# A gated attention block on one core: when reads of DRAM scratch are emitted, and large transfers cut in four

## The chip, the core and the metric

The kernel runs on one core of a Trainium2 chip. The metric is the device time of one execution in microseconds (us). TensorE (PE) multiplies matrices, VectorE (DVE) and ScalarE (ACT) work on tiles, GpSimd (POOL) masks, and SyncE (SP) does nothing but issue transfers (DMAs). Each engine takes its instructions in the order of the program. An instruction whose inputs aren't there holds everything behind it on its engine; for SP that means every later transfer.

## The reference, cut to what matters

`x` has 2 batches of 1024 tokens with 512 features. All arithmetic is float32.

```python
xn = layernorm(x)
q, k, v = xn @ Wq.T + bq, xn @ Wk.T + bk, xn @ Wv.T + bv      # 32 heads of 16
s = causal_softmax(q @ k.T / 4) @ v @ Wo.T + bo
f = xn @ W_base.T + b_base + 2-of-8 routed low-rank part (A, B, W_gate)
out = x + s * silu(f)
```

## The kernel before

**Tiling.** A chunk is 512 tokens, so there are 2 x 2 chunks (b, c). Four groups of eight heads (oc = 0 to 3) per chunk give 16 units (b, oc, c). A unit's attention is cut into steps; the list `plan` holds 144 of them. The loop at the end of `direct` records for each step n the scores (`s<-qT,kT`, line 1542), the product of the exponentials with the values for step n-1 (`av<-pt,v`, line 1594), the mask, and then calls `fill(n)`.

**Order.** Nothing is scheduled at run time. `fill(n)` records as many other matmuls (line 228) as the step's share allows, taken from a list of tasks with due steps; then it runs through `later`, a list of (step, function) pairs, and runs those whose step has come; then it steps the tasks that cost TensorE nothing (loads, sums of weights, layernorm); last, `issue_parts` records loads of weight blocks. So the recorded step of a DMA sets only its place on SP's queue. When it really starts depends on everything in front of it there.

**Weights in seven products.** Value, gate and output projections and most query-key projections use a scheme of seven products in place of eight. It needs sums of blocks of the weights. `combine_task` (line 583) loads a whole 1 MB matrix (`load_whole`, line 140), makes the four block sums in place on DVE (`four_sums`), and stores the result to DRAM scratch as one 1 MB DMA, `kept<-w_gate` (line 597). Later `issue_parts` (line 617) loads blocks of 256 KB one at a time: `w<-in_wb_dram` straight from the weight, `wt<-kept` from the scratch. `qk_weights_task` (line 621) does the same for the query-key weights of one oc: two loads of 256 KB (`load_qk`, line 123), pairing on ACT, sums on DVE, one 1 MB store `kept<-wqk` (line 646); for batch 1 the tile is read back (line 626). The `wqk` tiles share two buffers, so a third tile (`wqk2`) can only be loaded when the last product that reads the tile in its buffer (`wqk1`, in step 17) is done.

**Other trips through DRAM scratch.** Turning the normalized tokens: `scr<-sq` (line 301) and four reads `xnT<-scr` (line 308). Turning the routed activations: `hscr<-hsq` and `hwT<-hscr` (lines 980, 987). The softmax denominators of a unit: `den<-oT`, `den<-avs` (line 1029), `dens<-den` (line 1034), a reciprocal on DVE, `back<-rc` (line 1037), `avs<-back` (line 1054), and then on DVE `rb<-avs` and a product with `oT`. Each read waits on SP for its write. The step in which a read is recorded is a fixed number of steps after the write's: one for `place` and `spread`, one or two for `collect` and `merge`.

**Around step 12 to 22**, where the gate projection of chunk (0, 0) begins, SP's recorded order is: step 12 `w_gate`, the two loads of `wqk2`, first gate block `w11`; step 13 `hwT` four times, `kept<-wqk0`, block `w21`; step 15 `back<-rc`; step 16 `avs<-back` twice, `kept<-w_gate`; step 17 `wt2<-kept`, `wt3<-kept`; step 19 the copies of kT; step 20 those of qT and `wt1`. The products of the gate stand in the steps 19 (`p1`), 20 (`p2`), 21 (`p6`, which reads `wt2`) and on.

Of the kernel before, what the change touches and what calls it, by code (L numbers as in the profile page):

```python
# [18 lines left out]
P = 128  # L19
# [40 lines left out]

@with_exitstack
def attn_gated_block(ctx: ExitStack, tc: tile.TileContext, *args):

    nc = tc.nc
    flag = ctx.enter_context(tc.tile_pool(name="flag", bufs=1))
    sound = flag.tile([1, 1], I32, name="sound")
    with ExitStack() as direct_ctx:
        direct(direct_ctx, tc, sound, *args)
    n = nc.values_load(sound[0:1, 0:1])
    with tc.If(n < P * NF, preferred_fallthrough_block=False):
        with ExitStack() as general_ctx:
            general(general_ctx, tc, *args)


def direct(ctx, tc, sound, x, wq, wk, wv, wo, wb, wa, wg, wB, bq, bk, bv, bo, bb, out):
# [11 lines left out]
    act = Metered(nc.scalar, 0.22, 1274)  # L94
    NB, L, _ = x.shape
# [19 lines left out]
    for t in range(TT):  # L115
        nc.sync.dma_start(out=first[t], in_=x[0, t * P : (t + 1) * P, :])

    def load_qk(oc):


        t = sb.tile([P, 4 * KC, P], F32, tag="wqk", bufs=2, name=f"wqk{oc}")
        for n, src in enumerate((wq, wk)):
            nc.sync.dma_start(
                out=t[:, (2 + n) * KC : (3 + n) * KC],
                in_=src.rearrange("(kc p) o -> p kc o", p=P)[:, :, oc * P : oc * P + P],
            )
        return t
# [12 lines left out]
    def load_whole(src, name):  # L140

        t = sb.tile([P, KC, D], F32, tag="xnT", bufs=3, name=name)
        nc.sync.dma_start(out=t, in_=src.rearrange("(kc p) o -> p kc o", p=P))
        return t

    def load_b(src, name):
        t = cst.tile([P, D], F32, name=name)
        nc.sync.dma_start(out=t, in_=src.partition_broadcast(P))
        return t
# [13 lines left out]
    def load_rest():  # L163


        def by_rows(w):
            return w.rearrange("(kc p) o -> p kc o", p=P)

        for dst, src in (
            (wag_sb[:, :, 0:ER], by_rows(wa)),  # L170
            (wag_sb[:, :, ER:], by_rows(wg)),
            (wB_sb, wB),
            (bb_sb, bb.partition_broadcast(P)),
            (bo_sb, bo.partition_broadcast(P)),
        ):
            nc.sync.dma_start(out=dst, in_=src)
# [87 lines left out]
    def layernorm_task(b, c):  # L264


        xt = chunk_tile(b, c)
        for i in range(NS):
            i0 = c * C + i * P
            nc.sync.dma_start(  # L270
                out=xt[i * SQ : (i + 1) * SQ],
                in_=x[b, i0 : i0 + P].rearrange("(t r) d -> r t d", r=SQ),
            )
        if b == 0:
            load_rest()
        tiles = [xt[:, t] for t in range(TT)]
        for _ in range(3 if b else 1):
            yield WAIT
        s = yield from statistics(tiles, True)
        if b:  # L280
            yield WAIT
        for t in range(0, TT, 2):
            normalize(tiles[t : t + 2], s[0][:, t : t + 2], s[1][:, t : t + 2])
            yield PAUSE
        if b:
            yield WAIT
        xnT = sb.tile([P, KC, C], F32, tag="xnT", bufs=3, name=f"xnT_{b}_{c}")
        for k0 in range(0, KC, 2):
            sq = sb.tile([P, 2, NS, TT, SQ], F32, tag="sq", bufs=1, name="sq")
            for t in range(TT):  # L290
                yield PAUSE
                ve.transpose(
                    out=sq[:, :, :, t],
                    in_=tiles[t][:, k0 * P : (k0 + 2) * P].rearrange(
                        "p (k q d) -> p k q d", k=2, q=NS
                    ),
                )
            scr = dram.tile([NS, SQ, 2, NS, TT * SQ], F32, tag="scr", name="scr")

            def store(sq=sq, scr=scr):  # L300
                nc.sync.dma_start(
                    out=scr.rearrange("i d k q m -> (i d) (k q m)"),
                    in_=sq.rearrange("p k q t r -> p (k q t r)"),
                )

            def place(k0=k0, scr=scr):
                for q in range(NS):
                    nc.sync.dma_start(
                        out=xnT[q * SQ : (q + 1) * SQ, k0 : k0 + 2].rearrange(
                            "d k (i m) -> d k i m", i=NS  # L310
                        ),
                        in_=scr[:, :, :, q].rearrange("i d k m -> d k i m"),
                    )

            if not b:
                store()
                place()
                yield WAIT
                continue
            later.append((now[0] + b, store))  # L320
            later.append((now[0] + b + 1, place))
            for _ in range(0 if k0 else 1 + b):
                yield WAIT
        xnTs[b, c] = xnT
        turned_at[b, c] = now[0] + b
# [137 lines left out]
    def place_keys(kT, low):  # L463
        for par in range(2):
            nc.sync.dma_start(out=kT[1 - par :: 2, par].bitcast(F32), in_=low[par::2])
# [15 lines left out]
    def place_queries(qT):  # L481
        for par in range(2):
            both = qT[:, 2 * par : 2 * par + 2].bitcast(F32)
            nc.sync.dma_start(out=both[1 - par :: 2], in_=both[par::2])
# [82 lines left out]
    combined, kept_at, sums, sums_at, issued_at, ended = {}, {}, {}, {}, {}, [0]  # L567
    made = [0] * len(stages)
    qk_kept, qk_ready, qk_done = {}, {}, {}
# [13 lines left out]
    def combine_task(name, given=None):  # L583

        src, bias = weights[name]
        w = given or load_whole(src, f"w_{name}")
        for _ in range(0 if given else 3):
            yield WAIT
        at = {
            (i, j): w[:, 2 * i : 2 * i + 2, BK * j : BK * j + BK]  # L590
            for i in range(2) for j in range(2)
        }
        yield from four_sums(at, {int(t[1]): at[p] for t, p in IN_PLACE.items()})
        kept = dram.tile([P, KC, D], F32, tag=f"kept_{name}", bufs=1, name="kept")
        ve.tensor_tensor(bias[:, BK:D], bias[:, BK:D], bias[:, 0:BK], ALU.subtract)
        yield WAIT
        nc.sync.dma_start(out=kept, in_=w)
        combined[name], kept_at[name] = kept, now[0]

        for _ in range(2):  # L600
            yield WAIT

    def issue_parts():
        while issued[0] < len(parts) and issued[0] - used[0] < NWP:
# [3 lines left out]
            if part[0] == "t" and now[0] < kept_at.get(name, now[0]) + 1:  # L608
                return
            w = sb.tile([P, 2, BK], F32, tag="wp", bufs=NWP, name=f"w{part}")  # L610
# [6 lines left out]
            nc.sync.dma_start(out=w, in_=src)  # L617
# [3 lines left out]
    def qk_weights_task(n):  # L621

        oc = n % KC
        if n >= KC:
            wqks.append(sb.tile([P, 4 * KC, P], F32, tag="wqk", bufs=2, name=f"wqk{oc}"))
            nc.sync.dma_start(out=wqks[n], in_=qk_kept[oc])
        else:
# [17 lines left out]
            yield WAIT  # L645
            nc.sync.dma_start(out=qk_kept[oc], in_=w)
            for _ in range(2):
                yield WAIT
        qk_ready.setdefault(n, now[0] + 2)
# [179 lines left out]
    def gate_task(k):  # L829
# [18 lines left out]
        def final(i, j):  # L848
# [20 lines left out]
            def store():  # L869
                nc.sync.dma_start(out=block_of(kept)(i, j), in_=g(i, j))  # L870
# [9 lines left out]
    def out_task(k):  # L880
# [10 lines left out]
        def load():  # L891
            i, j = order[len(xts)]
            xts[i, j] = sb.tile([P, 2, BK], F32, tag="xr", name=f"xr_{b}_{c}_{i}{j}")
            nc.sync.dma_start(out=xts[i, j], in_=block(x, i, j))
            gts[i, j] = sb.tile([P, 2, BK], F32, tag="gr", name=f"gr_{b}_{c}_{i}{j}")
            nc.sync.dma_start(out=gts[i, j], in_=g(i, j))

        def final(i, j):
# [7 lines left out]
            def store():  # L906
                nc.sync.dma_start(out=block(out, i, j), in_=y(i, j))
# [10 lines left out]
    def routed_task(b, c):  # L918
# [60 lines left out]
        def store():  # L979
            nc.sync.dma_start(  # L980
                out=scr.rearrange("i d q m -> (i d) (q m)"),
                in_=sq.rearrange("p q t r -> p (q t r)"),
            )

        def place():
            for q in range(NS):
                nc.sync.dma_start(
                    out=hwT[q * SQ : (q + 1) * SQ].rearrange("d i t r -> d i (t r)"),
                    in_=scr[:, :, q].rearrange("i d m -> d i m"),
                )  # L990

        later.append((now[0] + 1, store))
        later.append((now[0] + 2, place))
        hwTs[b, c] = hwT
        turned_at[b, c, "h"] = now[0] + 1
# [20 lines left out]
    def post(n, b, oc, c, avs):  # L1016
# [10 lines left out]
        def leave():  # L1027
            for par, t in enumerate((o, avs)):
                nc.sync.dma_start(
                    out=den[par].rearrange("s j w -> s (j w)"), in_=t[HD - par :: HP]  # L1030
                )

        def spread():
            nc.sync.dma_start(out=dens[:, u], in_=den.rearrange("a s j w -> (a s j) w"))

        def give_back(rc):
            nc.sync.dma_start(
                out=back.rearrange("a s (j w) -> (a s j) w", w=W), in_=rc
            )
            later.append((now[0] + 1, collect))  # L1040
# [11 lines left out]
        def collect():  # L1052
            for par in range(2):
                nc.sync.dma_start(out=avs[HD - par :: HP], in_=back[par])
            later.append((now[0] + 2, finish))
# [10 lines left out]
        later.append((n + 3, spread))  # L1066
        if wait:
            patient.extend((merge, finish))
        later.append((n + 4 + wait, merge))

    def post_tile(b, oc, c, t, avs):
# [17 lines left out]
        if posted.count(t) == 2:  # L1089
            turns.append((now[0] + 1, lambda: turn_last(b, c, t)))  # L1090

# [19 lines left out]
    def bases_task(b, c):  # L1111

        xt = sb.tile([P, TT, D], F32, tag="xnT", bufs=3, name="x_last")
        nc.sync.dma_start(
# [17 lines left out]
    def finish_tile(b, c, t, po):  # L1132
# [4 lines left out]
        nc.sync.dma_start(out=out[b, i * P : (i + 1) * P, :], in_=y)  # L1137
# [172 lines left out]
    for b in range(NB):  # L1310
        for c in range(NC):
# [10 lines left out]
            turned_ = lambda u=(b, c): now[0] > turned_at.get(u, now[0]) + (3 if u[0] else 2)  # L1322
# [13 lines left out]
            if not b and not c:  # L1336
# [14 lines left out]
                for n in range(2 * KC):  # L1351
# [4 lines left out]
                            and len(qk_ready) >= n  # L1356
                        ),
# [77 lines left out]
    def fill(n):  # L1435
# [3 lines left out]
        now[0], begun_at = n, spent  # L1439
        within = 0 <= n < len(plan)  # L1440
# [54 lines left out]
        for x in [x for x in later if x[0] <= n]:  # L1495
            if x not in later or x[0] == n and x[1] in patient and enough():
                continue
# [617 lines left out]
```

## Time and profile before

| what | value |
| --- | --- |
| runs | 558.41, 559.28, 560.47 us; median 559.28 us |
| profiled execution | 560.55 us, of which the span of the trace is 558.8 us |
| ACT busy | 351.2 us (63%) |
| DVE busy | 332.7 us (60%) |
| transfers | 79.16 MB, mean 142 GB/s |
| largest group | `pt<-s` on ACT, 288 instructions of 1024 ns |

The span is the time from the first to the last instruction in the trace. The profiled execution is one of its own: its time lies 1.27 us above the median, and 1.75 us of it lie outside the span. "Busy" is the sum of an engine's instructions; a wait is idle time of an engine with the instruction that ended it. In the trace's lines, DVE and ACT instructions have line 56, since a helper (`Metered`) records them; they are told apart by their tiles.

### The profile page before, as it was taken

The numbers are of one execution on the slowest core, as the hardware profiler recorded it, in microseconds if no ns is written. First come the engines' busy times: TensorE is split into PE (matmuls) and PEld (weight loads), VectorE is DVE, ScalarE is ACT, GpSimd is POOL, SyncE is SP. The second block draws the span as 40 slices with busy tenths as digits, with TensorE's granted clock in tenths as the row PEclk, the third lists the DMA queues.
The fourth block names the chain that finished last, engine by engine and source line by source line (L and its number), as shares of the span: only waits on it lengthen the run. The fifth ranks groups of instructions, "written<-read, shape, count | busy, mean of one in ns | idle before, by whom it ended". The sixth has DMA issues, their size and how long they took to land.

```text
span 558.8 us, 19435 instructions
## 1 busy us (share of the span) xinstructions
PE 540.5 (97%) x8411; PEld 280.2 (50%) x8411; DVE 332.7 (60%) x693; ACT 351.2 (63%) x389; POOL 115.9 (21%) x248
## 2 busy tenths in 40 slices
PE   8999999959999999999999999999999999999993
PEld 8435444524445554444645554454545554455651
DVE  4435587137567675566549765585267553648833
ACT  2537754645777676756657755756667777776640
POOL 2203401010213530130213430120113331020500
PEclk9999999979999999999999999999999999999998
DMA  8634370565564555741575544641124221652311
GB/s 266 170 112 174 120 228 3 184 235 192 153 157 143 222 174 167 209 144 60 167 198 177 171 156 134 225 142 41 60 78 137 79 83 46 230 168 81 97 40 46
DMA packets 65198, 79.16 MB, mean 142 GB/s; under 512 B 9560, under 2 KB 52576, under 8 KB 63696
## 3 DMA queue, kind: packets, MB, share of 16 engines
q1 hardware_dynamic: 65088, 77.83, 43.5%
q8 instruction: 68, 1.11, 0.8%
q14 instruction: 26, 0.21, 0.1%
q10 hardware_dynamic: 16, 0.00, 0.0%
HBM read 46.39 MB, written 19.37 MB: 118 GB/s over the span
## 4 chain that ended last, share of the span: by engine, by line
PE 92%; DMA 3%; DVE 2%; ACT 1%; issue 0%; SPq 0%; POOL 0%; ACTq 0%; POOLq 0%; DVEq 0%
PE av L1594 25%; PE p L228 23%; PE s L1542 18%; PE q L228 13%; PE pv L228 2%; PE po L228 2%; PE ph L228 2%; PE pq L228 1%; PE pk L228 1%; DMA back<-rc 1%; ACT pt L56 1%; DMA kept<-w_gate 1%; PE warm L183 1%; DMA wqk<-in_wk_dram 1%; PE pq_first L351 1%; PE h L228 1%
## 5 line engine op out<-in xcount | busy, mean ns | idle before, releaser
L56 ACT ACTIVATE pt<-s 128x1024 f32<-128x1024 f32 x288 | 290.2, 1024 | 158.7 <-PE s L1542 149.0
L1570 POOL TENSOR_SCALAR_AFFINE_SELECT pt<-pt 128x256 f32<-128x256 f32 (+1 forms) x224 | 108.0, 497 | 416.9 <-ACT pt L56 416.1
L1594 PE MATMUL av<-pt,v 128*32 128x512 f32 (+3 forms) x1680 | 157.2, 469 | 0.2 <-DVE v L56 0.2
L1542 PE MATMUL s<-qT,kT 32*128 32x512 f32 (+3 forms) x1616 | 108.7, 365 | 0.7 <-ACT pt L56 0.5
L1542 PEld LDWEIGHTS s<-qT,kT 32*128 32x128 f32 x1616 | 62.4, 184 | 59.8 <-issue 35.3
L1594 PEld LDWEIGHTS av<-pt,v 128*32 128x32 f32 x1680 | 41.6, 109 | 55.0 <-issue 39.1
L228 PE MATMUL p<-wt,asum 128*32 128x256 f32 x960 | 59.9, 386 | 6.2 <-DMA wt<-kept 6.2
L228 PE MATMUL q<-asum,wqk 128*32 128x256 f32 x832 | 51.3, 379 | 0.6 <-DVE qf L56 0.6
L228 PEld LDWEIGHTS p<-wt,asum 128*32 128x32 f32 x960 | 31.8, 112 | 36.0 <-issue 12.2
L228 PE MATMUL q<-xnT,wqk 128*32 128x256 f32 x624 | 39.5, 379 | 0.0
L228 PEld LDWEIGHTS q<-asum,wqk 128*32 128x32 f32 x832 | 26.7, 110 | 24.6 <-issue 6.9
L56 DVE TENSOR_TENSOR g<-p,g 128x512 f32<-128x512 f32 x20 | 13.8, 689 | 31.6 <-PE p L228 31.5
L228 PEld LDWEIGHTS q<-xnT,wqk 128*32 128x32 f32 x624 | 20.2, 110 | 18.4 <-issue 6.6
L56 DVE SCALAR_TENSOR_TENSOR kf<-q,kf 128x256 f32<-128x256 f32 x39 | 16.5, 424 | 21.2 <-PE q L228 20.5
L228 PE MATMUL p<-w,xnT 128*32 128x256 f32 x448 | 27.9, 379 | 0.0
L228 PEld LDWEIGHTS p<-w,xnT 128*32 128x32 f32 x448 | 15.7, 110 | 10.3 <-issue 3.3
L228 PE MATMUL p<-w,asum 128*32 128x256 f32 x320 | 20.7, 379 | 0.0
L228 PEld LDWEIGHTS ph<-wag_sb,xnT 128*32 128x32 f32 x512 | 15.2, 110 | 3.9 <-issue 3.3
L228 PE MATMUL po<-wo,oT 128*32 128x512 f32 x128 | 16.5, 593 | 0.4 <-ACT oT L56 0.4
L228 PE MATMUL ph<-wag_sb,xnT 128*32 128x136 f32 x512 | 16.6, 279 | 0.0
L56 DVE TENSOR_TENSOR x<-p,x 128x512 f32<-128x512 f32 x15 | 10.3, 687 | 10.3 <-PE p L228 10.2
L56 DVE TENSOR_TENSOR qT<-qf,qT 128x512 fp32r<-128x512 f32 x15 | 10.3, 684 | 9.8 <-ACT qT L56 9.8
(145 smaller groups left out, 555.7 us busy)
## 6 DMA issues: line engine op xcount, KB each, us to landing
wt<-kept SPq DMA_DIRECT2D x40, 256.0 KB
qT<-qT SPq DMA_DIRECT2D x30, 256.0 KB
x<-in_x_dram SPq DMA_DIRECT2D x16, 256.0 KB
kept<-wqk SPq DMA_DIRECT2D x4, 1024.0 KB
wqk<-kept SPq DMA_DIRECT2D x4, 1024.0 KB
kT<-kf SPq DMA_DIRECT2D x30, 128.0 KB
scr<-sq SPq DMA_DIRECT2D x6, 512.0 KB
xnT<-scr SPq DMA_DIRECT2D x24, 128.0 KB
```

Of the source, the lines that this page charges most:

```text
L56: return getattr(self.engine, name)(*args, **named)
L183: nc.tensor.matmul(warm[:, n % 4 * P : n % 4 * P + P], lhsT=ident, rhs=ident, start=True, stop=True)
L228: nc.tensor.matmul(o[j : j + 32], lhsT=lhsT[:, j : j + 32] if len(lhsT.shape) == 2 else lhsT[:, j // 32], rhs=rhs, start=start, stop=stop,)
L351: nc.tensor.matmul(ps[:, cols], lhsT=w[:, k, :], rhs=xnT[:, k, cols], start=k == 0, stop=k == KC - 1)
L1542: nc.tensor.matmul(ss[s // 2][:, s % 2, col : col + w], lhsT=keys[rows, kt % TT * P : kt % TT * P + P], rhs=q[rows, halves * par + half_, ...
L1570: nc.gpsimd.affine_select(out=d, in_=d, compare_op=ALU.is_ge, fill=0.0, base=0, pattern=[[0, d.shape[1]], [1, P]], channel_multiplier=-1,)
L1594: nc.tensor.matmul(avs_now[par][32 * s : 32 * s + 32, q0 : q0 + w], lhsT=vs[b, kt][:, h * VS - HD * par : h * VS - HD * par + HP], rhs=pt[ ...
```

## The change

**An estimate of the landing.** A new class `Queue` stands around SP. It adds up the bytes of all DMAs at 2.8e5 bytes per us, from the planner's own clock; `landing()` is that sum plus 1.8. `landed(f, cap)` notes this estimate for a function that reads what was just written, and `fill` keeps the function back in `later` until the estimate has passed or step `cap` has come. It is used for `place` (both kinds), `spread`, `merge`, `collect` and `finish`. `issue_parts` holds back blocks `wt` of a matrix in the same manner, up to three steps after its store.

**Cuts.** `load_whole` for the gate and output weights is cut into four DMAs of 256 KB, recorded one per step. The store `kept<-wqk` is cut into four, one per step, and a later load of `wqk` waits (in the recording) until the store in its way is recorded whole.

**Steps.** `combine_task` waits six steps instead of three between load and sums.

```diff
+class Queue:
+    def __init__(self, engine, rate=2.8e5):
+        self.engine, self.now, self.free, self.rate = engine, 0.0, 0.0, rate
+    def dma_start(self, out, in_):
+        n = 4
+        for k in out.shape:
+            n *= k
+        self.free = max(self.free, self.now) + n / self.rate
+        return self.engine.dma_start(out=out, in_=in_)
+    def landing(self):
+        return self.free + 1.8
...
-    def load_whole(src, name):
+    def load_whole(src, name, apart=None):
         t = sb.tile([P, KC, D], F32, tag="xnT", bufs=3, name=name)
-        nc.sync.dma_start(out=t, in_=src.rearrange("(kc p) o -> p kc o", p=P))
+        if apart is None:
+            sp.dma_start(out=t, in_=src.rearrange("(kc p) o -> p kc o", p=P))
+        else:
+            for kc in range(KC):
+                apart.append((
+                    now[0] + 1 + kc,
+                    lambda kc=kc: sp.dma_start(out=t[:, kc], in_=src[kc * P : kc * P + P]),
+                ))
         return t
...
-        w = given or load_whole(src, f"w_{name}")
-        for _ in range(0 if given else 3):
+        w = given or load_whole(src, f"w_{name}", later)
+        for _ in range(0 if given else 6):
             yield WAIT
...
         combined[name], kept_at[name] = kept, now[0]
+        kept_lands[name] = sp.landing()
...
             if part[0] == "t" and now[0] < kept_at.get(name, now[0]) + 1:
                 return
+            if part[0] == "t" and kept_lands[name] > clock[0] + 1.0 and now[0] < kept_at[name] + 3:
+                return
...
-            yield WAIT
-            nc.sync.dma_start(out=qk_kept[oc], in_=w)
-            for _ in range(2):
+            for i in range(4):
                 yield WAIT
+                part = slice(i * KC, i * KC + KC)
+                sp.dma_start(out=qk_kept[oc][:, part], in_=w[:, part])
+            qk_stored.add(n)
...
+                            and len(qk_stored) > min(n, KC + 1) - 2
...
-        later.append((now[0] + 1, store))
-        later.append((now[0] + 2, place))
+            landed(place, now[0] + 3)
...
+    def landed(f, cap, at=None):
+        needs[f] = sp.landing(), cap
+        later.append((now[0] + 1 if at is None else at, f))
...
+            lands, cap = needs.get(x[1], (0.0, 0))
+            if lands > (begins if x[1] in patient else clock[0] + 1.0) and n < cap:
+                continue
```

## The prediction, made before the changed kernel had run

> **What bounds the kernel now.** I read the shares of the engines first, then what TensorE waited for, then its timeline at the one long wait, then the chain of waits and SP's own waits behind it.
>
> ```profile
> PE 540.5 (97%) x8411; PEld 280.2 (50%) x8411; DVE 332.7 (60%) x693; ACT 351.2 (63%) x389; POOL 115.9 (21%) x248
> ...
> PE 92%; DMA 3%; DVE 2%; ACT 1%; issue 0%; SPq 0%; POOL 0%; ACTq 0%; POOLq 0%; DVEq 0%
> ```
>
> PE is busy for 97% of the span and idle for 18.3 us in all. A change that leaves PE's instructions alone can win from those 18.3 us only.
>
> ```profile
> PE p L228 <- DMA wt<-kept: 6.2, 1, 6.2
> PE warm L183 <- POOL mhalf L192: 1.4, 1, 1.4
> PE q L228 <- DVE qf L56: 0.6, 1, 0.6
> ```
>
> PE's own waits: one of 6.2 us for a gate block read back from scratch, and nothing else over 0.6 us once the warm-up is past. Of the rest, 7.8 us lie after the last matmul (551.0 to 558.8) and 2.0 us in the first 14.6 us.
>
> ```profile
> 110.01 0.80 PE L1542 MATMUL s<-qT,kT 32*128 32x384 f32 x16
> 110.74 1.06 PE L1594 MATMUL av<-pt,v 128*32 128x512 f32 x8
> 111.63 0.61 PE L228 MATMUL p<-w,xnT 128*32 128x256 f32 x8
> 112.06 1.04 PE L228 MATMUL p<-wB_sb,hwT 128*32 128x256 f32 x16
> 119.31 1.93 PE L228 MATMUL p<-wt,asum 128*32 128x256 f32 x16 [6.21 <-DMA wt<-kept]
> 121.17 1.23 PE L1542 MATMUL s<-qT,kT 32*128 32x256 f32 x16
> ...
> 113.10:119.30 6.20, 0.00 (x1) 0.02 (x1) 3.53 (x12) 3.58 (x5) 1.53 (x4) 0.91 0.43 148
> 119.30:125.10 5.80, 5.79 (x60) 2.97 (x64) 0.00 (x0) 1.74 (x2) 0.63 (x1) 0.50 0.94 314
> ```
>
> The first lines are PE's timeline (start, length). It stops at 113.10 and goes on at 119.31. The last two are stretches of time; the seventh figure is the granted clock: 0.50 for the 5.8 us after the stop. There 16 matmuls of the form `p` take 1.93 us, where the 16 before the stop took 1.04; with the `s`, `av` and `p` groups behind them (1.23, 1.94, 2.41 us; the same forms take 0.75, 1.07, 1.91 around 203 us) the slow clock costs (1.93+1.23+1.94+2.41) - (1.04+0.75+1.07+1.91) = 2.7 us. The clock record in the trace has it fall at 118.23, 5.13 us after PE stopped. So the stop is worth 6.2 + 2.7 = 8.9 us.
>
> ```profile
> 97.50 0.91 PE q L228 x16
> ...
> 98.43 0.38 SPq L123
> ...
> 98.86 4.63 DMA wqk<-in_wk_dram
> ...
> 103.56 5.90 DMA back<-rc
> ...
> 109.51 0.50 SPq L1054
> ...
> 110.64 5.81 DMA kept<-w_gate
> ...
> 116.47 2.70 DMA wt<-kept
> ...
> SPq L123 <- PE q L228: 19.3, 1, 19.3
> ```
>
> These are pieces of the chain of waits (start, length) and, last, one of SP's own waits (total, count, longest). SP stood for 19.3 us at the load of `wqk2`, because the buffer is that of `wqk1`, which `q4` of step 17 reads last (done at 98.41). All that SP had behind it started then: `wqk2`, `w11`, `hwT`, `kept<-wqk0` (1 MB), `w21`, `back<-rc`; `avs<-back` waited for `back`; `kept<-w_gate` stood behind it, although its sums were ready at 94.05; `wt2` waited for that store.
>
> **The change, part by part.** The built programs have the same PE rows and the same ACT rows in the same order (5108 rows on PE); DVE has the same 676 instructions, some moved; SP has 388 DMAs for 370 (+3 for `w_gate`, +3 for `w_out`, +12 for four stores `kept<-wqk`). 18 more issues of 0.38 us (row of `kept`) are 7 us of SP's time, hidden where SP waits anyway (35 waits for `p` alone come to 81.0 us).
>
> *What the estimate moves.* Only a few reads change step: `xnT<-scr` of chunk (1, 0) from 45 to 46 and 48 to 49, `avs<-back` from 88 to 89, `dens<-den` of the first unit behind the copies of kT, `wt2` and `wt3` of the gate from 17 to 20. The `xnT` reads were held on SP by their writes anyway (issued 206.5 and 217.1; steps 46 and 49 begin at 206.2 and 217.0), and PE needs the last of them at 228.3, 5.3 us after it landed at 223.0. I take 0; if a whole step (3.4 us) were added to the landing, 1.9 us would still be left.
>
> *The gate chain.* SP's new order is: `w_gate` pieces 1 and 2, `wqk2`'s two loads (step 14), piece 3, `back<-rc`, a piece of `kept<-wqk0`, piece 4, `avs<-back`, a last piece of `wqk0`, kT, `kept<-w_gate` (step 19), qT, `wt2`, `wt3`. The hold is still there: `wqk2` waits for `q4` as before, and half of `w_gate` is now behind it. In front of the hold went `w11`, `w21` and `hwT`, none of which PE waited for. On DVE the sums moved from step 15 to 18, behind `rb<-avs`. So the sums, ready early before, are now a link of the chain. On the clock of the old trace, from the release at 98.43:
>
> - `back<-rc` takes the fourth place after the release, where `hwT` was issued: 100.26 (old: 103.56). In front of it lie `wqk2` (landed 98.86 + 4.63 = 103.49) and 256 KB of `w_gate`; the trace's semaphore updates show `w11`, as large and in that place, at 104.43, and `back` 0.20 after the DMA in front of it (108.17, 15 of 16 shares 108.37). So `back` lands at 104.6 (old 109.46).
> - `avs<-back` to `rb<-avs`: 111.94 - 109.51 = 2.43, so 107.1. `rb` and `oT`: 113.40 - 111.94 = 1.46, so 108.5.
> - four sums of `w_gate`, old row 2.86 us: 111.4. The store starts then (old 110.64).
> - the store: 5.81 gives 117.2. `wt2`, issue to first matmul: 119.31 - 116.47 = 2.84, so 120.0.
>
> The early sums also made PE wait 0.6 us for `qf` just ahead of `q4`; that goes, and PE and the release both come 0.6 earlier. PE stops at 112.5 and goes on at 119.4, against 119.31: **+0.1 us**. The gain of 4.9 us on `back` is spent on 2.4 + 1.5 + 2.9 us of work that was not in the chain. The stop is 6.9 us, so the slow clock stays.
>
> Bounds. Low: `back` lands with `wqk2` at 103.5 (-1.1), and the store takes 3.91, for 15 of its 16 shares had landed at 114.55 and one at 116.45, while a 16 KB instruction fetch ran from 113.44 (-1.9): PE goes on at 116.4, a stop of 3.9 us, shorter than the 5.13 after which the clock fell, so -2.9 - 2.7 = -5.6. High: `back` straggles by 1.1 as before (109.46 for 108.37), and the copies of qT, now in front of `wt2`, cost their issue, 1.23: +2.4. I take 5.81 for the store: the fetch came 0.34 us after PE stopped, PE's instructions are the same, and the store again lies across that moment.
>
> A rule bears on the clock. The Trainium skill, "TensorE: Matmul & The Clock Gate", section "What's actually happening", says the clock is halved after an idle window of about 3.4 us, windows running free. The row has 5.13 us. By the row a stop of 5.0 us keeps full clock; by the rule it may lose it, and the first rival below would then win 1.8 us, not 4.5.
>
> *Cut stores.* `kept<-wqk` in pieces lets `dens<-den` and `wt4` pass sooner (they landed at 80.5 and 80.3, behind a 1 MB store); `wt4` was wanted only at 84.6. 0. A rule speaks against cutting: "DMA: Bandwidth & Descriptors", section "Rules for kernel authors", wants at least 1 MiB per DMA for bandwidth. Here a 256 KB load behind others added 0.94 us, so four in a row come to 3.8 us, and the whole load of `w_gate` took 5.88 (78.54 to 84.42): by the rows the cut costs no bandwidth, by the rule it would cost some, and PE waits for none of these in either case.
>
> *The output weights.* The load goes from step 34 to 35-38, the sums from 37 to 41, the store `kept<-w_out` from 38 to 42. Its first reader is `wt2`, issued at 243.8; 0. But the store now lies in front of the copy of qT for unit (0, 2, 1), which landed at 201.76 and is read by PE in step 46 at 206.2. That 4.4 us of slack is the cover; the store took 6.0 us (181.83 to 187.86), so without any overlap it would cost 1.6 us. The store starts some 3 us ahead of the copy, so 0.
>
> Sum: 560.55 + 0.1 for the profiled execution, which lies 1.27 us above the median; the median goes from 559.28 to **559.4 us**.
>
> **The rivals.**
>
> *The straggler doesn't recur (faster).* Store 3.91: PE goes on at 117.5 after 5.0 us, the clock holds by a hair, -1.8 - 2.7: 554.8 us. For it: the straggler hangs on when a fetch falls. Against it: the fetch follows PE.
>
> *The change does what it is named for: the block is there when PE wants it (faster).* Then 8.9 + 0.6 go: 549.8 us. Against it is the hold of 19.3 us, which no part of the change removes; even the low bound leaves 3.9 us.
>
> *The rings stay full in the gate chain (slower).* `back` needs 5.90 us from its issue as it did (landing 106.2, +1.6), and `wt2` stands behind the data of the two qT copies as well as their issue (+1.25): PE goes on at 122.2, +2.9, 562.2 us. It decides from the point where `back` lands after 106. (The qT copies' data: 121.06 to 122.31 in the semaphore updates.) For it: three transfers of 256 KB still go in front of `back` and two more right behind. Against it: beside `wqk2`, 1.75 MB lay between the release and `back` (`w11`, `hwT`, `kept<-wqk0`, `w21`), now 0.25 MB.
>
> **How the numbers follow.** A measurement of this kernel tells about 0.5% (2.8 us) from no change. The forecast, a stop of about the same length (556.5 to 562.1), gets 0.55. The first rival 0.20, the second 0.07; the third, with all else that could make a new stall, 0.18. The range runs from the low bound, 553.7, to about the third rival's time, 562.0: the second rival lies below, half of the third above. Faster 0.27, same 0.55, slower 0.18.
>
> **What would show it.** Right: PE still waits 6 to 7 us for `wt<-kept` at about 112.5; SP still waits some 19 us or less for `q` before `wqk2`, released at about 97.8; the four sums of `w_gate` stand after `rb<-avs`, at about 108; the wait for `qf` is gone; clock 0.5 after the stop. Wrong: `kept<-w_gate` issued before 108, a stop under 5 us, or a wait of PE above 1 us elsewhere, first of all in steps 42 to 46.

## The result, and the profile after

The changed kernel takes 558.85 us (median of 20 runs, 557.08 to 560.37); the kernel before, measured beside it, also 558.85 us (20 runs, 557.16 to 560.47). The ratio is 0.9997, 95% interval 0.9986 to 1.0009: no change that can be told. The profiled execution has a span of 557.1 us.

In its trace every DMA that SP issues bears line 72 (the helper that keeps the estimate), and PE's lines are renumbered: L253 was L228, L1587 was L1542, L1639 was L1594. The first fence is the page's list of busy times, the second what PE and then SP waited for (total, times, longest).

```profile
PE 539.0 (97%) x8411; PEld 278.9 (50%) x8411; DVE 333.0 (60%) x693; ACT 351.2 (63%) x389; POOL 116.0 (21%) x248
```

```profile
PE p L253 <- DMA wt<-kept: 6.7, 1, 6.7
...
SPq L72 <- PE q L253: 16.8, 3, 7.5
```

PE is as busy as before, and its one long wait is the same wait for the same block: 6.7 us where it was 6.2. The wait for `qf` (0.6 us) is gone. The time did not go elsewhere. What led to the wait did change. These are pieces of the chain of waits (start, length, what):

```profile
103.43 0.70 DVE kf L56
...
104.39 1.81 DMA avs<-back
...
106.24 0.76 DVE rb L56 x2
...
107.63 0.90 DVE w_gate L56
...
110.84 5.38 DMA kept<-w_gate
116.21 0.02 issue
116.23 2.73 DMA wt<-kept
118.96 0.14 issue
119.10 1.94 PE p L253 x16
```

Before, the chain ran over SP's queue into the store `kept<-w_gate`, whose sums had been ready since 94.05. Now the sums of `w_gate` are a link, behind `rb`, which stands behind `avs<-back` and `kf`. SP's timeline (start, length, issues) shows the other half:

```profile
97.72 0.38 SPq L72 DMA_DIRECT2D wqk<-in_wq_dram  x1
...
99.81 0.38 SPq L72 DMA_DIRECT2D back<-rc  x1
...
100.71 0.43 SPq L72 DMA_DIRECT2D w_gate<-in_wb_dram  x1
103.84 1.03 SPq L72 DMA_DIRECT2D avs<-back  x2
...
110.84 0.33 SPq L72 DMA_DIRECT2D kept<-w_gate  x1
112.44 1.68 SPq L72 DMA_DIRECT2D qT<-qT  x2
116.23 1.40 SPq L72 DMA_DIRECT2D wt<-kept  x3
```

`back<-rc` was issued at 103.56 and is now issued at 99.81, and `avs<-back` follows at 103.84 where it was 109.51. Yet the store still starts at 110.84 (110.64 before), because `rb`, `oT` and the four sums came between. In the two stretches of the stop and after it the seventh figure is the granted clock:

```profile
112.41:119.10 6.69, 0.00 (x0) 0.03 (x1) 1.96 (x9) 2.96 (x5) 1.53 (x4) 0.86 0.70 267
119.10:124.90 5.80, 5.80 (x68) 3.00 (x72) 0.00 (x0) 1.75 (x2) 0.63 (x1) 0.57 0.60 173
```

### The profile page after: what moved, and what is told of

Read it like the earlier page. It is cut to its first block, busy times and chain, and to the rows that moved or that the text cites. A ratio compares the mean times of both kernels' runs of the same rounds, so it can differ in the third digit from the quotient of the medians.

```text
span 557.1 us, 19461 instructions
## 1 busy us (share of the span) xinstructions
PE 539.0 (97%) x8411; PEld 278.9 (50%) x8411; DVE 333.0 (60%) x693; ACT 351.2 (63%) x389; POOL 116.0 (21%) x248
## 4 chain that ended last, share of the span: by engine, by line
PE 91%; DVE 3%; DMA 2%; ACT 2%; issue 1%; SPq 0%; DVEq 0%; ACTq 0%
PE av L1639 25%; PE p L253 22%; PE s L1587 18%; PE q L253 14%; PE ph L253 3%; PE pv L253 2%; PE po L253 2%; PE pk L253 1%; PE pq L253 1%; ACT pt L56 1%; DMA kept<-w_gate 1%; PE pq_first L378 1%; PE h L253 1%; DVE w_gate L56 1%; DVE g L56 1%
## 5 line engine op out<-in xcount | busy, mean ns | idle before, releaser
L1639 PE MATMUL av<-pt,v 128*32 128x512 f32 (+3 forms) x1680 | 156.6, 469 | 0.3 <-DVE v L56 0.2
L1587 PE MATMUL s<-qT,kT 32*128 32x512 f32 (+3 forms) x1616 | 108.7, 365 | 0.7 <-ACT pt L56 0.5
L1587 PEld LDWEIGHTS s<-qT,kT 32*128 32x128 f32 x1616 | 62.4, 184 | 59.8 <-issue 34.6
L1639 PEld LDWEIGHTS av<-pt,v 128*32 128x32 f32 x1680 | 41.3, 109 | 55.2 <-issue 39.5
L253 PE MATMUL p<-wt,asum 128*32 128x256 f32 x960 | 59.5, 384 | 6.7 <-DMA wt<-kept 6.7
L253 PE MATMUL q<-asum,wqk 128*32 128x256 f32 x832 | 51.1, 379 | 0.0
L253 PEld LDWEIGHTS p<-wt,asum 128*32 128x32 f32 x960 | 31.8, 111 | 36.1 <-issue 19.5
L253 PE MATMUL q<-xnT,wqk 128*32 128x256 f32 x624 | 39.5, 379 | 0.0
L253 PEld LDWEIGHTS q<-asum,wqk 128*32 128x32 f32 x832 | 26.8, 110 | 23.7 <-issue 6.9
L253 PEld LDWEIGHTS q<-xnT,wqk 128*32 128x32 f32 x624 | 20.2, 110 | 18.5 <-issue 6.6
L253 PE MATMUL p<-w,xnT 128*32 128x256 f32 x448 | 27.4, 379 | 0.0
L253 PE MATMUL p<-w,asum 128*32 128x256 f32 x320 | 20.7, 379 | 0.0
L253 PEld LDWEIGHTS p<-w,xnT 128*32 128x32 f32 x448 | 14.9, 110 | 10.6 <-issue 3.3
L253 PEld LDWEIGHTS ph<-wag_sb,xnT 128*32 128x32 f32 x512 | 15.2, 110 | 3.9 <-issue 3.3
L253 PE MATMUL po<-wo,oT 128*32 128x512 f32 x128 | 16.5, 593 | 0.4 <-ACT oT L56 0.4
L253 PE MATMUL ph<-wag_sb,xnT 128*32 128x136 f32 x512 | 16.6, 279 | 0.0
```

What stands on the lines that cost most here:

```text
L253: nc.tensor.matmul(o[j : j + 32], lhsT=lhsT[:, j : j + 32] if len(lhsT.shape) == 2 else lhsT[:, j // 32], rhs=rhs, start=start, stop=stop,)
L1587: nc.tensor.matmul(ss[s // 2][:, s % 2, col : col + w], lhsT=keys[rows, kt % TT * P : kt % TT * P + P], rhs=q[rows, halves * par + half_, ...
L1639: nc.tensor.matmul(avs_now[par][32 * s : 32 * s + 32, q0 : q0 + w], lhsT=vs[b, kt][:, h * VS - HD * par : h * VS - HD * par + HP], rhs=pt[ ...
```

## The experiments

The question was whether the hold of SP at `wqk2` makes the gate block late in both kernels, and what each part of the change does alone. Each kernel was timed against the kernel before in runs of its own (558.99, 559.31 or 559.35 us); ratios are to those.

### Moving the load out of the hold, in the kernel before

```
-  (20, 13, 24, 28)[n] if n < KC else -9, qk_weights_task(n), 0.0, after=9,
+  (20, 13, 24, 28)[n] if n < KC else -9, qk_weights_task(n), 0.0, after=18 if n == 2 else 9,
```

> The kernel before, with one edit: the load of wqk2 is recorded in step 18 (after q4, which reads its buffer last) and no longer in step 12. Theory A (the hold of SP at wqk2 is what makes the gate block late, in both kernels): SP no longer waits 19 us for q; kept<-w_gate is issued near 95 us, soon after its sums; PE's wait of 6.2 us for wt<-kept and the 2.7 us of slow clock behind it are gone, the 0.6 us for qf stays; about 550 us (8.9 less than before), 19 us less on no engine. Rival B (the block is late because its read is emitted too early, and the hold is only what the waiting shows up on): the stall stays near 6 us, time about 559. Rival C (wqk2, now later, is missed by its sums and by q of step 31): a new wait of PE near 170-190 us and less than 4 us gained.

Measured: 552.14 us, ratio 0.9872 (0.985 to 0.9894). PE waits for nothing above 1.4 us (that one is in the warm-up), so the new wait of rival C did not come. SP's timeline of this kernel:

```profile
94.68 0.33 SPq L597 DMA_DIRECT2D kept<-w_gate  x1
98.60 1.89 SPq L617 DMA_DIRECT2D wt<-kept  x2
100.54 0.46 SPq L123 DMA_DIRECT2D wqk<-in_wq_dram  x1
```

The store goes 16 us earlier and the stall is gone: for the kernel before, theory A holds. The gain is 6.9 us by the medians, not the 8.9 that the profiled execution of before had led me to write; that execution, 560.55 us, was one of the longer ones.

### The same edit in the kernel after

> The kernel after, with the same edit (wqk2's load in step 18). Theory A: the chain back, rb, oT, sums of w_gate, store, wt2 is as long as before, but its first link no longer waits for the release at 97.7 us; kept<-w_gate is issued near 103 us (110.8 in after), the block lands near 112 us and PE's wait for wt<-kept falls from 6.7 us to under 1; about 550 us. Rival B (the later sums alone make the block late, whatever SP does): kept<-w_gate is issued after 108 us, PE waits 4 us or more, 556 us or more.

Measured: 555.12 us (553.74 to 559.34), ratio 0.9918 (0.9891 to 0.9946). Theory A missed. Rival B is nearer: its store after 108 us and its wait of 4 us came, its 556 us did not. The profiled run is the one of 559.34 us: it also waited 1.7 us for the first load of `wqk` and had one stretch of half clock at 9 us, so its axis is 2.6 us late against that of after. The gate stall in it is 4.0 us. DVE's timeline (in brackets the idle time before, and what ended it):

```profile
106.05 0.69 DVE L56 TENSOR_TENSOR kf<-kf,kT 128x512 f32<-128x512 f32 x1 [4.77 <-ACT kT L56]
106.66 0.01 DVE L56 LOAD_MASK_SELECT rb<-avs  x1
106.66 0.75 DVE L56 STREAM_SHUFFLE rb<-avs 128x512 f32<-128x512 f32 x1
107.45 0.69 DVE L56 TENSOR_TENSOR oT<-oT,rb 128x512 f32<-128x512 f32 x1
108.06 2.98 DVE L56 TENSOR_TENSOR w_gate<-w_gate 128x512 f32<-128x512 f32 x4
```

`avs<-back` was issued at 94.08, so `avs` was there long before, and so was `w_gate`. DVE nevertheless stood for 4.77 us at `kf<-kf,kT`, which waits for ACT, with `rb`, `oT` and the sums behind it. The store was issued at 111.07, 108.5 on the axis of after: 2.3 us earlier than in after, not the 7.8 expected. So the hold is only the first of two things that make the block late in the kernel after. The second is where the sums stand in DVE's stream.

### The load of w_gate whole again, in the kernel after

```
-  w = given or load_whole(src, f"w_{name}", later)
-  for _ in range(0 if given else 6):
+  w = given or load_whole(src, f"w_{name}", later if name == "out" else None)
+  for _ in range(0 if given else 6 if name == "out" else 3):
```

> The kernel after, with w_gate loaded whole and summed three steps after its load, as before the change; w_out stays cut, and so do the stores and the estimate. The hold of SP at wqk2 stays. My account of the change (it frees back<-rc by 4.9 us and gives that back by putting the sums of w_gate behind rb and oT): with the sums early again, kept<-w_gate is issued near 105 us instead of 110.8, PE's wait for wt<-kept is near 1 us, the clock does not fall, and the wait of 0.6 us for qf returns: about 551 to 552 us. Rival (the hold alone decides, the place of the sums does not matter): PE waits 6 to 7 us, about 559 us. Rival (the 1 MB load, whole, is again in the way of something in front of PE): between, 554 to 557 us.

Measured: 551.23 us, ratio 0.986 (0.9836 to 0.9885). PE waits 0.6 us for `qf` and not at all for `wt`; the clock does not fall. SP's timeline:

```profile
99.08 0.38 SPq L72 DMA_DIRECT2D wqk<-in_wq_dram  x1
...
100.33 0.45 SPq L72 DMA_DIRECT2D back<-rc  x1
103.02 1.04 SPq L72 DMA_DIRECT2D avs<-back  x2
104.15 0.39 SPq L72 DMA_DIRECT2D kept<-w_gate  x1
```

The hold is still there, to 99.08, and the store follows `avs<-back` at once, because its sums are done. That is 6.7 us earlier than in the kernel after. The cut of this one load, with the six waits that go with it, is what keeps the change from a gain of 7.8 us (551.23 against 558.99 for the kernel before, timed beside it). The two were not tried apart, and three waits would not do with the cut: the last of the four pieces is recorded four steps after the task begins, and the sums must come behind it.

### Only the order on DVE, in the kernel after

```
-  landed(finish, min(now[0] + 3, last), now[0] + 2)
+  landed(finish, min(now[0] + 3, last), now[0] + (3 if now[0] == 16 else 2))
```

> The kernel after; the only thing moved is on DVE: rb<-avs and oT of the first unit come one step later, behind the four sums of w_gate, not ahead of them. SP's hold stays. kept<-w_gate is then issued near 108 us instead of 110.8 (the sums no longer wait for avs), wt2 lands near 116.4, and PE stops for about 4.0 us instead of 6.7. If the clock falls only some 5 us after PE stops, as the traces of before and after have it (5.1 and 4.9 us), it stays full here: 2.7 us less wait and 2.7 us less slow clock, about 553.5 us. If it falls after a free-running window of about 3.4 us, as the Trainium skill has it (TensorE: Matmul & The Clock Gate, What's actually happening), it may fall here too: about 556 us. If the sums were not a link of the chain: no change, 559 us.

Measured: 553.99 us, ratio 0.9903 (0.9881 to 0.9925); the store was issued at 106.94. PE stopped for only 3.03 us, since the store took 4.1 us and no share of it came late. The clock fell all the same, at least in the profiled run, which is the longest of the four (553.40 to 555.65 us). The shortest has a mean granted clock of 0.996 against 0.992 there and may have kept it, so the median near 553.5 us does not decide between the two branches. The windows of the stop and after it, in the profiled run:

```profile
112.40:115.43 3.03, 0.00 (x0) 0.03 (x1) 1.83 (x7) 0.97 (x2) 0.66 (x2) 0.83 0.70 214
115.43:121.20 5.77, 5.77 (x60) 2.96 (x64) 0.00 (x0) 1.72 (x2) 0.64 (x1) 0.50 0.60 174
```

So 5.1 us is no threshold. The last section has more on this.

### Both edits: no hold, and the sums ahead of rb

The kernel after with the edits of the second and the fourth experiment.

> The kernel after with both earlier edits: wqk2's load recorded in step 18, and rb and oT of the first unit one step later, behind the four sums of w_gate. With the hold gone and rb out of the way, what is left in front of the sums on DVE is the subtraction of kf in step 18, which waits for ACT's kT (104 to 104.5 us in the other kernels). If the place of the sums in DVE's stream is itself the last link: sums 104.5 to 107.4, kept<-w_gate 107.4 to 111.4, wt2 behind the copies of qT at 112, first matmul at 114.8: PE waits 2 to 2.5 us where after waited 6.7, about 552 to 553.5 us, and up to 556 if the clock falls. If only the hold and rb stood in the way: no wait of PE over 1 us, 551 us.

Measured: 554.12 us (552.29 to 554.48), ratio 0.9905 (0.9882 to 0.9927). The profiled run is that of 552.29 us. DVE's timeline and then PE's:

```profile
103.41 0.69 DVE L56 TENSOR_TENSOR kf<-kf,kT 128x512 f32<-128x512 f32 x1 [4.77 <-ACT kT L56]
104.02 2.86 DVE L56 TENSOR_TENSOR w_gate<-w_gate 128x512 f32<-128x512 f32 x4
```

```profile
114.73 1.07 PE L253 MATMUL p<-wt,asum 128*32 128x256 f32 x16 [2.36 <-DMA wt<-kept]
```

The first account holds: with the hold and `rb` both out of the way, the sums still wait behind `kf` until 104.02, and PE stops for 2.36 us, here at full clock (16 matmuls in 1.07 us). The place of the sums in DVE's stream, three steps later by the six waits, is a link by itself. That the three other runs, 1.8 to 2.2 us longer, lost the clock is argued from their mean granted clock (0.992 to 0.995, against 0.997 in the profiled one), not shown.

### The parts of the change, one at a time

The estimate alone (the kernel after with whole loads and the whole store):

```
-  w = given or load_whole(src, f"w_{name}", later)
-  for _ in range(0 if given else 6):
+  w = given or load_whole(src, f"w_{name}")
+  for _ in range(0 if given else 3):
...
-  for i in range(4):
-      yield WAIT
-      part = slice(i * KC, i * KC + KC)
-      sp.dma_start(out=qk_kept[oc][:, part], in_=w[:, part])
-  qk_stored.add(n)
+  yield WAIT
+  sp.dma_start(out=qk_kept[oc], in_=w)
+  for _ in range(2):
+      yield WAIT
...
-  and len(qk_stored) > min(n, KC + 1) - 2
```

> The kernel after without either cut: whole loads, whole stores, the estimate of landings alone. SP holds at wqk2 as before, with w11, hwT, kept<-wqk0 and w21 behind it. If the estimate does nothing to the gate block (my prediction): PE waits some 6 us for wt<-kept, clock 0.5 behind it, about 559 us. If the estimate does what it is named for: reads no longer stand on SP in front of other work, the stall is under 3 us, 553 us or less. If the estimate costs something elsewhere (xnT<-scr of chunk (1, 0) goes from step 48 to 49): PE waits above 1 us near 220 us, 560 us or more.

Measured: 558.54 us (557.42 to 563.69), ratio 1.0003 (0.9979 to 1.0028). The estimate alone does nothing to the time. The profiled run (557.42 us, the shortest of ten) stopped for 4.2 us: `kept<-w_gate` was issued at 110.97 as ever, but landed after 3.90 us.

The cut query-key stores alone, in the kernel before:

```
...
-  yield WAIT
-  nc.sync.dma_start(out=qk_kept[oc], in_=w)
-  for _ in range(2):
-      yield WAIT
+  for i in range(4):
+      yield WAIT
+      part = slice(i * KC, i * KC + KC)
+      nc.sync.dma_start(out=qk_kept[oc][:, part], in_=w[:, part])
+  qk_stored.add(n)
...
+  and len(qk_stored) > min(n, KC + 1) - 2
```

> The kernel before with the cut query-key stores alone (four pieces, and the next load of wqk only once they are out); w_gate and w_out are loaded whole, nothing is estimated. By the built programs wqk2's load goes to step 14, and SP's order in steps 8 to 24 is that of the kernel after with w_gate loaded whole. Theory D: PE's wait for wt<-kept is gone and the time is that of that kernel, 551 to 552 us. Rival (the estimate of landings is what gains): the stall of 6 us stays, about 559 us.

Measured: 552.08 us, ratio 0.9879 (0.9844 to 0.9914). `back<-rc` was issued at 100.30 and the store of `w_gate` at 104.28, as in the kernel after with the load whole. One of the four runs took 1340.81 us, and nothing on record says why; the other three took 551.69 to 552.14 us.

The cut load of `w_gate` alone, in the kernel before (with the changed kernel's `load_whole`):

```
-  w = given or load_whole(src, f"w_{name}")
-  for _ in range(0 if given else 3):
+  w = given or load_whole(src, f"w_{name}", later if name == "gate" else None)
+  for _ in range(0 if given else 6 if name == "gate" else 3):
```

> The kernel before with the cut load of w_gate alone (four pieces, its sums six steps after the first and not three). wqk2's load is then in step 12, ahead of all four pieces, so all of w_gate lies behind the hold, and the sums stand behind rb on DVE. From rows of before: back<-rc is issued behind three more pieces of 0.94 us, 105 to 106.4 us, lands 3 us later than before's 109.46, so rb at 114.7, sums until 119, the store of 4 to 5.8 us, wt2 2.8 us: PE goes on at 126 to 128 and stops 13 to 15 us: 566 to 569 us, if the cut load is what takes back what the cut stores win. Rival (the place of the sums costs nothing, the block only waits for back): kept<-w_gate some 3 us later than before's 110.64 and about 562 us.

Measured: 570.59 us, ratio 1.0211 (1.0183 to 1.0239), a little above the expected 566 to 569. The chain of that kernel:

```profile
99.03 4.00 DMA wqk<-in_wk_dram
...
103.12 0.04 ACT wqk L56
...
104.14 1.93 ACT pt L56 x2
...
113.49 0.76 DVE rb L56 x2
...
114.88 0.69 DVE w_gate L56
...
123.49 6.61 DMA wt<-kept
```

The sums come at 114.88, behind `rb`, as expected. What I had not counted: with this edit the pairing of `wqk2` on ACT came earlier in ACT's order. It stood 8.57 us waiting for that load, with `pt` (the exponentials) behind it, and PE waited 6.3 us for `pt` besides 8.4 us for `wt`. So the time came near the expected one by other terms than the single stop of 13 to 15 us. PE's order changes in steps 50 to 57 too, so the 11.3 us are not those of the cut alone.

All cuts without the estimate: the diff of the change without `Queue`, `landed` and what they decide (SP's order in steps 7 to 42 is that of after):

> The kernel after without the estimate of landings: both loads and the stores cut, six waits, all else recorded as before. SP's order in steps 7 to 42 is that of after. If the cuts alone make what after is: PE waits 6 to 7 us for wt<-kept, kept<-w_gate near 110.8 us, about 559 us. If the estimate takes a part in it: another stall, and a time off by more than 2.8 us.

Measured: 558.68 us, ratio 0.9982 (0.9968 to 0.9997), with the stop of after:

```profile
PE p L235 <- DMA wt<-kept: 6.9, 1, 6.9
```

So the change is its cuts: the stores' cut wins 7.2 us by itself, the load's cut with its six waits gives that back, the estimate has no part in it.

### Only the step of one load

In the kernel before, `after=14 if n == 2 else 9` in the line of the first experiment: the step at which the cut stores let `wqk2` load.

> The kernel before, with one edit: the load of wqk2 is recorded in step 14, where the changed kernel has it, and no longer in step 12. Nothing is cut and nothing is estimated; TensorE's order is that of before. SP still stands at wqk2 until q4 of step 17 is done (about 98 us), but w11, hwT, kept<-wqk0 and w21 are in front of the hold now, so back<-rc is issued right behind wqk2. Theory D (what the change gains, it gains by moving this load two steps): back<-rc near 100.3 us (103.56 before), kept<-w_gate near 104 (110.64), no wait of PE for wt<-kept above 1 us: 551 to 552 us. Rival (the cut of the stores is needed too, since a 1 MB store in one piece still lies in front of something): PE waits 2 us or more, 554 to 559 us.

Measured: 551.59 us, ratio 0.9873 (0.9845 to 0.99). The time is as theory D had it, but the way is another. SP's timeline, and what SP waited for:

```profile
90.28 0.38 SPq L123 DMA_DIRECT2D wqk<-in_wq_dram  x1
...
91.31 1.41 SPq L1037 DMA_DIRECT2D back<-rc  x1
...
96.21 0.39 SPq L597 DMA_DIRECT2D kept<-w_gate  x1
```

```profile
SPq L123 <- DMA kept<-wqk: 5.6, 1, 5.6
```

There is no wait for `q` at this load. `wqk2` waits only until the store of `wqk0`'s sums is out. By the addresses in the built programs `wqk2` lies in the buffer of `wqk1` in before, after, the whole load, the cut stores and the cut load, and in that of `wqk0` here and in both kernels with the load in step 18. The store of `wqk0` is recorded in step 13: a load recorded in step 12 finds that buffer taken and gets the one that `q4` reads until step 17; a load recorded in step 14 finds it free. With cut stores the last piece of `wqk0` is recorded in step 16 (after) or 17 (the cut stores alone), so step 14 finds it taken again, and the hold stays. That the recorded store decides the choice is read off these programs; it fits these eight. It is not the whole rule: in the best version, next, that piece is recorded in step 17 and the load in step 18, and `wqk2` still lies in the buffer of `wqk1`. There the load's turn comes only at 99.29, and SP does not stand at it.

### The best version

The whole load and `wqk2` in step 18 together:

> The kernel after with w_gate whole and wqk2's load in step 18. Either edit alone takes a part of the stall or all of it (551.2 us and 555.1 us). With the whole load PE already waits for nothing but 0.6 us for qf, so the second edit should win nothing: 551.2 us within 1 us, kept<-w_gate near 95 us instead of 104. If the 0.6 us or something after it hangs on the hold too: 550.5 us or less.

Measured: 551.27 us, ratio 0.9855 (0.9831 to 0.9878); the store was issued at 94.41. It wins nothing over 551.23, as expected: PE has no stall left to give. Several ways lead to the same floor of 551 to 552 us, the smallest of them one number in the kernel before. Not tried: a third buffer for `wqk`.

## Why the prediction was right

The forecast was 559.4 us, with a stop of about the same length; measured were 558.85 us and 6.69 us. Its chain stands term by term (the prediction counted on the old clock, so 0.6 is taken off behind `q4`):

| step | predicted | measured |
|---|---|---|
| SP released at `wqk2` | 97.8 | 97.72 |
| `back<-rc` issued | 99.7 | 99.81 |
| `back` landed (`avs<-back` issued) | 104.0 | 103.84 |
| `rb` starts | 106.5 | 106.24 |
| sums of `w_gate` done, store issued | 110.8 | 110.84 |
| store landed, `wt2` issued | 116.6 | 116.23 |
| PE goes on | 119.4 | 119.10 |
| stop | 6.9 | 6.69 |

- **What bounds the kernel** (a stop of 6.2 us and 2.7 us of slow clock, 8.9 in all): the mechanism is shown by five kernels without the stall. By the medians it is worth 6.9 to 8.1 us; the 8.9 belonged to one execution. That a change can win "from those 18.3 us only" is wrong, for the slow clock's 2.7 us stand in PE's busy time: that fell from 540.5 us to 538.2 with the load in step 18.
- **"The hold is still there"**: right; but SP came to it later, so its longest wait for `q` is 7.5 us, not 19.3. In front of it SP waited 3.4 us for a store of `wqk`.
- **The gain of `back` spent on the sums**: right, and shown both ways: sums early with the hold, 551.23 us; hold gone with the sums late, 555.12.
- **A link left out**: in front of `rb`, DVE stood at `kf<-kf,kT` for ACT until 103.43, which the chain does not have. It cost nothing only because `avs` came later (106.21). With `back` earlier it became the next limit (the load in step 18, and both edits).
- **The store, 5.81**: measured 5.38. One share was late again, but not for the reason given. I had it that the instruction fetch follows PE's stop; it came at 111.4, 1.0 us ahead of the stop. It fell into the store none the less, which is luck: with the estimate alone no fetch fell in, the store took 3.90 us and the stop was 4.16.
- **The clock** ("by the row a stop of 5.0 us keeps full clock"): wrong. Stops of 3.03, 4.01 and 4.16 us lost it, and one of 2.36 us did not. This step failed. It entered the low bound and the first rival, which gave 2.7 us too much to a stop of 3.9 to 5.0 us; the forecast itself has a longer stop and did not need it.
- **Cut stores "0"**: right for what that paragraph priced (nothing else became late), but the large effect of the cut, moving `wqk2` by two steps, stood in my chain as a given order and I had not seen that this is the cut's doing, nor that it alone is worth 7.2 us.
- **Estimate, `xnT` reads, output weights, 0**: shown by the estimate alone (1.0003), and by 551.23 with the estimate and the cut of `w_out` against 552.08 without either. The slack for `w_out` was misread: of the two copies of qT the second landed at 204.55 (not 201.76), 1.7 us ahead of its reader and not 4.4. In after it landed at 204.07, 1.1 us ahead, and PE did not wait.
- **"By the rows the cut costs no bandwidth"**: not shown by those rows. The 0.94 us are what one load adds behind others, the 5.88 us the whole time from issue to landing; in after one piece of 256 KB took 4.2 us from issue to landing (100.71 to 104.91). PE waited for none of them.
- **Rivals**: the straggler did recur. The second rival was argued away by the hold ("even the low bound leaves 3.9 us"), but the kernel with the whole load has the hold and no stall: it was the later sums that ruled it out. The third did not come: `back` landed at 103.84, well ahead of 106.

## What to carry to other kernels

When a change frees one link of a late chain, look at what else the same change put behind that link: here a transfer came 5.7 us earlier and four sums that had been ready early came 17 us later, on an engine that works in order behind a wait of its own. A load that holds a queue may owe it to the buffer that it was given: ask which of the buffers will be free first at the place where the load is recorded, and move the load past the store that keeps the better one. And test the parts of a change one by one even where the whole does nothing; this one hid 7 us.

## What the runs showed of the hardware

**The clock goes by a free-running grid.** In every trace here the record of the granted clock changes only at multiples of 3.413 us from its first entry (112.64 us, 33 of them, from the first entry to the fall in before; the low stretches inside the kernels are 6.83 or 3.41 us). The table takes the 3.41 us that end at the fall and says how much of it PE was idle; ends of matmuls are modelled, so a few hundredths are uncertain.

| kernel | PE stopped | clock low | idle in the window before the fall |
|---|---|---|---|
| before | 113.10 to 119.31 | 118.23 to 125.06 | 3.41 |
| after | 112.41 to 119.10 | 117.28 to 124.11 | 3.41 |
| after, load in step 18 | 115.01 to 119.02 | 118.16 to 124.99 | 3.15 |
| all cuts, no estimate | 112.81 to 119.75 | 115.94 to 122.77 | 3.13 |
| the estimate alone | 113.59 to 117.75 | 118.94 to 122.35 | 2.22 |
| sums ahead of `rb` | 112.40 to 115.43 | 114.42 to 121.25 | 2.02 |
| both edits | 112.37 to 114.73 | not | 1.55 at most |

At this stop, windows with 1.46, 1.72 and 1.94 us idle (after, before, the estimate alone: each the window ahead of the one in the table) did not make it fall, one with 2.02 did. That is no limit for other places: in the trace of after with the load in step 18, falls also followed a window with 1.70 us idle near the start (5.52 to 8.93) and one with 1.98 us at the end (548.24 to 551.65). So idle time alone does not decide, and what else does is not shown. A stop shorter than one window, here of 3.03 us, can cost the clock, depending on where it lies on the grid, and the fall can come when PE is at work again: with the estimate alone it came 1.2 us after PE had gone on. These are that kernel's stretches:

```profile
113.59:117.75 4.16, 0.00 (x1) 0.03 (x1) 2.29 (x6) 3.32 (x4) 1.54 (x4) 1.00 0.55 182
117.75:118.90 1.15, 1.15 (x20) 0.62 (x24) 0.74 (x4) 0.27 (x2) 0.00 (x0) 1.00 0.99 374
118.94:122.30 3.36, 3.36 (x40) 1.79 (x40) 0.38 (x2) 1.50 (x2) 0.64 (x1) 0.50 0.82 268
```

The Trainium skill, "TensorE: Matmul & The Clock Gate", section "What's actually happening", has the free-running window of 3413 ns, and the traces agree with it against my reading of 5.13 us as a threshold. It speaks of an idle window; here windows idle for 1.70 and 2.02 of their 3.41 us were enough.

**One of a DMA's 16 shares can be late when an instruction fetch falls in.** The landing of a DMA shows in the trace as 16 semaphore updates, here called its shares. By their times:

```
kernel            transfer         issued   15 shares   last share   16 KB fetch at
before            kept<-w_gate     110.64   114.55      116.45       113.4
after             kept<-w_gate     110.84   114.77      116.21       111.4
after             qT<-qT (first)   112.44   115.34      116.80       (same)
estimate alone    kept<-w_gate     110.97   114.87      114.87       none, 107.8 to 119.9
sums ahead of rb  kept<-w_gate     106.94   111.08      111.08       111.2
sums ahead of rb  qT<-qT (first)   110.14   112.42      113.81       (same)
whole load        kept<-w_gate     104.15   108.18      110.11       105.2
```

The late share costs 1.4 to 1.9 us, on the transfer under way or on the one behind it, and those of the table with no fetch in or just ahead of them have none. With `wqk2`'s load in step 18 of the kernel after, the fetch came 0.33 us before its store had landed (114.72; 115.05): that store had no late share, but the copies of `qT` behind it had. Of the 59 stores of 1 MB in one piece in the thirteen traces, 17 had such a fetch begin before their fifteenth share had landed. In 7 of these the last share came 1.0 to 2.0 us behind the fifteenth; in the other 42 it never came more than 0.4 us behind. So each late share had a fetch, but most fetches brought no late share. That the fetch is the cause is not shown; no run moved a fetch on purpose.
